# An attention layer and a layer of 160 experts on one core: one after the other, or in bursts between head groups

## The chip, the cores and the metric

The kernel runs on one core of a Trainium2 chip. The core has a tensor engine (PE, whose weight loads the profile lists as PEld), a vector engine (DVE), a scalar engine (ACT), a general engine (POOL) and a sync engine (SP), which here only issues transfers. [...] The metric is the device time of the kernel in microseconds (us): 3245.87 us as the median of three runs (3244.12 to 3246.43). Smaller is better.

## The reference

Sixteen batches of 512 tokens with 128 channels pass through one transformer block. Shifts, scales and gates of both halves come from a small conditioning vector. First comes causal attention with 16 heads of 8 channels, and then a mixture of 160 experts, of which each token takes 8, and one shared expert. All is in float32.

```python
mod = (_silu(L0_c) @ L0_wmod).reshape(L0_c.shape[0], 6, 1, -1)
sa, ca, ga, sb, cb, gb = (mod[:, k] for k in range(6))      
h = _layernorm(x) * (1 + ca) + sa
# attention: qkv = h @ qkv_w.T + qkv_b, rotary q and k, causal softmax, out @ proj_w.T + proj_b
x = x + ga * attention(h)
h = _layernorm(x) * (1 + cb) + sb
probs = sigmoid(h @ router_w.T + expert_bias)                 # 160 experts, inner width 64
top_w, top_idx = top_k(probs, 8)
top_w = 2.5 * top_w / (sum(top_w) + 1e-9)
routed = sum over the 8: top_w * (silu(h @ w_gate[e].T) @ w_down[e].T)
x = x + gb * (routed + silu(h @ w_gate_shared.T) @ w_down_shared.T)
```

## The kernel before

**Attention.** `attention` runs over 64 head groups: 16 batches, each with four groups of four heads. `prepare` makes one batch ready two batches ahead: normalized rows, transposes, q, k and v, the rotary turn, and q and k split into three bfloat16 parts, which go out to DRAM (`parts`). `fetch` brings the parts of one head group back, repeated over the partitions, into one of four pairs of tiles (`NREP = 4`, `qrep` and `krep`), with six transfers on SP. For each head group the program writes, in turns, the scores of this group with the causal mask (L363, L370), their exponentials on ACT (L373), the scores of the group two ahead (L317, L324) for their row maxima on DVE (`maxima`, L329), and the weighted sum of v (`weighted`, L382). `shift` puts the maxima back as extra rows of q. `collect` divides by the sums, and `project` applies the output weights and the gate and adds to x. The scores live in three PSUM tiles of two banks (tag `s`). One bank (tag `o`) serves the small transposes, one (`av`) the weighted sums.

**Experts.** `experts` runs when the attention is over, and its pools take over PSUM: four banks with tag `m`, and two tiles of two banks with tag `u`. The 16 batches form four groups of four. For each batch `route` normalizes, finds the top eight experts and computes the shared expert. `place` sorts a group's tokens by expert: every pair of experts gets whole blocks of 128 slots, at most `NK` = 207 blocks a group. For every block of 128 tokens POOL scatters the rows to their slots in DRAM (`xg`), eight indirect transfers a block (L740). `compute` then takes four blocks of slots at a time, a quad, through five stages: `load` from `xg`, `turn` (transposes, L782, copied by DVE, L784), `up` (the gate weights of the pair and two router columns, L790; then DVE's small operations L801 to L806, the Silu on ACT, L809, and the weighting, L810 and L812), `back` (transposes, L819, copied by ACT, L821) and `down` (L826, copied by ACT, L834, and stored to `yg`). Different stages of five quads are written in each step. Gate and down weights of all experts (`wg`, `wd`) lie in SBUF. PE reads the numbers of the expert pairs into registers. `combine` gathers each token's eight rows back by eight indirect transfers on POOL (L848), sums them (L858), weights them and stores the result.

```python
for i in range(-2, NQ + 3):
    for stage, q in (("load", i + 2), ("turn", i), ("up", i - 1), ("back", i - 2), ("down", i - 3)):
        if 0 <= q < NQ:
            getattr(quads[q], stage)()
    next(beside, None)
drain(beside)
```

What sets the order: the program is unrolled, and the generators of this loop decide what stands beside what. `beside` is the placing of the next group and the routing of the one after it, later also the combining of the group before. The scatter of `x` slots needs a cleared `xg`; 18 zero fills (L119) stand on SP before the first parts are stored.

Of the kernel before, what the change touches and what calls it, by code (L numbers as in the profile page):

```python
# [19 lines left out]
NB = 16  # L20
# [9 lines left out]
NREP = 4  # L30
# [5 lines left out]
NGR = 4  # L36
GB_ = NB // NGR
TB = GB_ * NBLK
TOPK = 8

NK = TOPK * TB + NC - 1
# [7 lines left out]
OFF = [sum(S - P * a for a in range(i)) for i in range(NBLK + 1)]  # L49
# [3 lines left out]
def block_kernel(ctx: ExitStack, tc: tile.TileContext, t: dict, out: bass.AP):  # L53
    nc = tc.nc

    const = ctx.enter_context(tc.tile_pool(name="const", bufs=1))

    stats = ctx.enter_context(tc.tile_pool(name="stats", bufs=4))
    early = ExitStack()
    early_pool = early.enter_context(tc.tile_pool(name="early", bufs=1))  # L60

    def load(name, shape, dt=FP, rows=False, pool=const):
        dst = pool.tile(shape, dt, tag=name, name=name)
        nc.sync.dma_start(out=dst, in_=t[name].partition_broadcast(P) if rows else t[name])
        return dst


    x = const.tile([P, NB * NBLK, D], FP, tag="x", name="x")

    def load_x(eng, b):  # L70
        eng.dma_start(
            out=x[:, b * NBLK : (b + 1) * NBLK, :],
            in_=t["x"][b].rearrange("(n p) d -> p n d", p=P),
        )

    load_x(nc.gpsimd, 0)
    cT = load("cT", [D, NB])
    wmod = load("wmod", [D, 6 * D], pool=early_pool)
    c = SimpleNamespace(
        ident=load("ident", [P, P]),  # L80
        wqk=load("wqk", [D, 2, 2, D], pool=early_pool),
        bqk=load("bqk", [D, 2, 2], pool=early_pool),
        wv=load("wvT", [D, D], pool=early_pool),
        bv=load("bv", [P, D], rows=True, pool=early_pool),
        turn=load("turn", [D, 2, S], pool=early_pool),
        identb=load("identb", [P, P], BF, pool=early_pool),
        mask_q=load("mask_q", [P, P], BF, pool=early_pool),
        mask_k=load("mask_k", [P, P], BF, pool=early_pool),
    )
    for b in range(1, NB):  # L90
        load_x(nc.sync if b % 2 else nc.gpsimd, b)
    c.wproj = load("wprojT", [D, D], pool=early_pool)
# [11 lines left out]
    c.blocks = load("blocks", [P, NK])  # L104
    c.slots = load("slots", [P, NK])
    c.wg = const.tile([D, NC, P + 2], FP, tag="wg", name="wg")
    for k in range(8):
        sl = slice(k * NC // 8, (k + 1) * NC // 8)
        nc.gpsimd.dma_start(out=c.wg[:, sl, :], in_=t["wgT"][:, sl, :])


    xg = [tc.dram_tile([NK * P, D], FP, name=f"xg{i}") for i in range(2)]
    yg = [tc.dram_tile([NK * P, D], FP, name=f"yg{i}") for i in range(2)]
    zeros = early_pool.tile([P, 1, D], FP, tag="zeros", name="zeros")
    nc.gpsimd.memset(zeros, 0.0)
    for rows in xg:
        view = rows.rearrange("(p n) d -> p n d", p=P)
        for k in range(0, NK, 23):
            nc.sync.dma_start(out=view[:, k : k + 23, :], in_=zeros.broadcast_to([P, 23, D]))  # L119

    eps = const.tile([P, 1], FP, tag="eps", name="eps")
    nc.vector.memset(eps, EPS)


    mod = const.tile([D, 6, NB], FP, tag="mod", name="mod")
    with tc.tile_pool(name="pmod", bufs=1, space=PSUM) as pp, tc.tile_pool(
        name="smod", bufs=1
    ) as sp:
        sc = sp.tile([D, NB], FP)
        nc.scalar.activation(sc, cT, AF.Silu)  # L130
        pm = pp.tile([D, 6, NB], FP)
        for k in range(6):
            nc.tensor.matmul(
                pm[:, k, :], lhsT=wmod[:, k * D : (k + 1) * D], rhs=sc, start=True, stop=True
            )
        nc.vector.tensor_copy(mod, pm)
        for k in (CA, CB):
            nc.vector.tensor_scalar(mod[:, k, :], mod[:, k, :], 1.0, None, ALU.add)
        for k in (GA, GB):
            g = mod[:, k, :]  # L140
            sign = sp.tile([D, NB], FP)
            nc.vector.tensor_scalar(sign, g, 0.0, 2.0, ALU.is_ge, ALU.mult)
            nc.vector.tensor_scalar(sign, sign, 1.0, None, ALU.subtract)
            mag = sp.tile([D, NB], FP)
            nc.vector.tensor_scalar(mag, g, -1.0, None, ALU.mult)
            nc.vector.tensor_tensor(mag, mag, g, ALU.max)
            nc.vector.tensor_scalar(mag, mag, 0.25, None, ALU.max)
            nc.vector.tensor_tensor(g, sign, mag, ALU.mult)


    stat1 = const.tile([P, NB * NBLK, 2], FP, tag="stat1", name="stat1")
    stat2 = const.tile([P, NB * NBLK, 2], FP, tag="stat2", name="stat2")

    def moments(stat, n):
        six = stats.tile([P, 6], FP, tag="six", name="six")
        nc.vector.bn_stats(six, x[:, n, :])
        nc.vector.bn_aggr(stat[:, n, :], six)

    def invert(stat, sl):
        nc.scalar.activation(stat[:, sl, 1], stat[:, sl, 1], AF.Sqrt, bias=eps)  # L160
        nc.vector.reciprocal(stat[:, sl, 1], stat[:, sl, 1])

    def normalized(pool, stat, n):

        xn = pool.tile([P, D], FP, tag="xn", name="xn", bufs=4)
        nc.vector.tensor_scalar(
            xn, x[:, n, :], stat[:, n, 0:1], stat[:, n, 1:2], ALU.subtract, ALU.mult
        )
        return xn

    def first_statistics(blocks):
        for n in range(blocks.start, blocks.stop):
            moments(stat1, n)
        invert(stat1, blocks)

    first_statistics(slice(0, NBLK))
    attention(tc, c, x, mod, (stat1, stat2), (first_statistics, moments, normalized))
    early.close()
    invert(stat2, slice(0, NB * NBLK))
    experts(tc, c, t, x, mod, stat2, (xg, yg), out)  # L180


def drain(steps):
    for _ in steps:
        pass


def heads_of(v):
    return v[:, :, 0 : H * (HD + 1)].rearrange("p n (h e) -> p n h e", e=HD + 1)


def attention(tc, c, x, mod, statistics, normalization):

    nc = tc.nc
    stat1, stat2 = statistics  # L200
    first_statistics, moments, normalized = normalization
    with ExitStack() as ctx:
        sb = ctx.enter_context(tc.tile_pool(name="attn", bufs=2))
        pads = ctx.enter_context(tc.tile_pool(name="pads", bufs=1))
        ps = ctx.enter_context(tc.tile_pool(name="attn_ps", bufs=1, space=PSUM))

        def bank2():
            return ps.tile([P, 2, S], FP, tag="s", name="s", bufs=3)

        def bank(shape=None, dt=FP):  # L210
            return ps.tile(shape or [P, S], dt, tag="o", name="o", bufs=1)


        reps = []
        for i in range(NREP):
            pair = [
# [791 lines left out]
```

## Time and profile before

| | |
|---|---|
| median of three runs | 3245.87 us |
| the profiled execution, its own time | 3244.43 us |
| its span, from the first to the last instruction | 3243.1 us |
| mean granted clock of PE | 0.766 |
| busy: PE, DVE, POOL, ACT | 1758.9, 1439.5, 1061.9, 906.9 us |
| first exponentials' scores, and the last (L363) | 167.4 and 1147.4 us |
| scatters (L740) and gathers (L848) | 512 and 512, 977 and 968 ns each |
| quads | 208 (4 x 52) |
| loads of ACT's function tables | 36, 1283 ns each |

The profile is one execution. Busy time is the time in which an engine ran an instruction; matmuls are pipelined, so that several of them can overlap and a busy PE is not one at its peak. The rows of 40 digits cut the span into 40 slices of 81 us, each digit a busy share in tenths. The table of stretches gives, for chosen stretches of time, the busy time of each engine with its number of instructions in brackets, then the granted clock of PE, the share of the DMA engines and GB/s. The timeline lists single instructions: start, duration, engine, line, operation, output <- inputs, and in square brackets how long the engine was idle ahead of it and what ended that. "SPq" is a transfer issued by SP. The list of waits gives, for an instruction and what released it, the sum in us, how often, and the longest.

### The profile page before, as it was taken

Reading aid. Unit: us, or ns where it says so; the run is one execution under the profiler, and the core shown is the slowest. Engines: PE = TensorE matmul, PEld = TensorE weight load, DVE = VectorE, ACT = ScalarE, POOL = GpSimd, SP = SyncE. Lnnn points to the kernel's source line nnn. Section 1 sums busy time; section 2 is a strip of 40 time slices with the busy share of each in tenths; the row PEclk is TensorE's granted clock in tenths of the full one; section 3 lists DMA queues with packets and bytes.
Section 4 is the critical chain, followed back from the end, with each engine's and each line's share of the span. In section 5 each row is a group of like instructions: output and inputs, shape, how many; then the busy total and the mean of one; then the engine's idle time right before and its main releaser. Section 6 shows DMA issues by size and latency. Waiting matters only on the chain.

```text
span 3243.1 us, 37324 instructions
## 1 busy us (share of the span) xinstructions
PE 1758.9 (54%) x12772; PEld 1234.9 (38%) x12772; DVE 1439.5 (44%) x3719; ACT 906.9 (28%) x1448; POOL 1061.9 (33%) x1079
## 2 busy tenths in 40 slices
PE   2189889888988863141288235138137228336700
PEld 1044444444444432031187235137136117336600
DVE  4156666666766553140176344026336115235522
ACT  1044444544444441010055012015013004113400
POOL 3000000000000006726701664650662670662176
PEclk8589999999999965565599667559568569668855
DMA  9811111111111011111245234124234125334421
GB/s 285 232 53 48 58 52 46 59 52 48 52 59 50 31 65 43 51 57 60 71 140 151 71 94 120 55 77 127 54 90 134 62 68 157 82 93 132 136 58 49
DMA packets 348310, 277.55 MB, mean 86 GB/s; under 512 B 28032, under 2 KB 319584, under 8 KB 348128
## 3 DMA queue, kind: packets, MB, share of 16 engines
q1 hardware_dynamic: 313568, 200.56, 20.6%
q0 software_dynamic: 34560, 74.60, 8.0%
q8 instruction: 109, 1.79, 0.2%
q14 instruction: 73, 0.60, 0.1%
HBM read 142.54 MB, written 131.73 MB: 85 GB/s over the span
## 4 chain that ended last, share of the span: by engine, by line
PE 37%; another core or an unknown queue 20%; issue 13%; DVE 11%; ACT 7%; POOL 6%; SPq 4%; DMA 2%; ACTq 0%; DVEq 0%; POOLq 0%
PE av L382 8%; POOL got L848 6%; PE m L826 4%; PE u L790 4%; ACT pT L373 4%; PE s L317 4%; PE s L363 3%; PE m L819 3%; SPq L119 3%; PE m L782 2%; DVE s L858 2%; PE s L248 2%; DVE mins L329 1%; PE o L397 1%
## 5 line engine op out<-in xcount | busy, mean ns | idle before, releaser
L848 POOL DMA_INDIRECT got<-yg,idx x512 | 495.6, 968 | 668.9 <-DMA yg<-y 359.0
L740 POOL DMA_INDIRECT xg<-h,idx x512 | 500.1, 977 | 405.9 <-issue 152.6
L329 DVE TENSOR_REDUCE mins<-s 128x2 f32<-128x1024 f32 (+3 forms) x512 | 418.6, 820 | 316.7 <-PE s L324 309.0
L373 ACT ACTIVATE pT<-s 128x1024 f32<-128x1024 f32 (+3 forms) x512 | 357.3, 703 | 280.9 <-PE s L370 273.3
L790 PE MATMUL u<-wg,xT 128*128 x1656 | 261.9, 303 | 315.7 <-DVE xT L784 126.8
L819 PE MATMUL m<-ident,su 128*128 128x128 f32 x828 | 149.1, 310 | 417.6 <-DVE su L812 186.4
L790 PEld LDWEIGHTS u<-wg,xT 128*128 128x128 f32 x1656 | 234.7, 215 | 326.0 <-issue 234.2
L282 POOL TENSOR_TENSOR rot<-rot 128x1024 f32<-128x1024 f32 x16 | 37.7, 2353 | 931.5 <-DVE rot L257 931.5
L821 ACT COPY hwT<-m 128x512 f32<-128x512 f32 x208 | 121.5, 584 | 757.5 <-remote 439.3
L317 PE MATMUL s<-krep,qrep 96*128 96x512 bf16 (+3 forms) x1024 | 262.5, 308 | 105.5 <-DMA krep<-parts 92.4
L382 PE MATMUL av<-pT,v 128*32 128x256 f32 (+3 forms) x2048 | 276.2, 444 | 1.3 <-ACT pT L373 1.3
L819 PEld LDWEIGHTS m<-ident,su 128*128 128x128 f32 x828 | 105.1, 159 | 446.1 <-issue 386.1
L826 PE MATMUL m<-wd,hwT 128*128 x1656 | 255.3, 305 | 21.3 <-issue 20.3
L363 PE MATMUL s<-qrep,krep 128*128 128x512 bf16 (+3 forms) x1024 | 258.2, 306 | 12.1 <-DVE mins L329 11.9
L784 DVE COPY xT<-m 128x512 f32<-128x512 f32 x208 | 141.7, 682 | 237.6 <-remote 163.1
L826 PEld LDWEIGHTS m<-wd,hwT 128*128 128x128 f32 x1656 | 237.3, 221 | 23.0 <-issue 20.9
L858 DVE TENSOR_REDUCE s<-got 128x128 f32<-128x1024 f32 x64 | 120.9, 1889 | 245.4 <-DMA got<-yg,idx 242.3
L324 PE MATMUL s<-mask_q,identb 128*128 128x128 bf16 x1024 | 208.9, 223 | 0.0
L370 PE MATMUL s<-mask_k,identb 128*128 128x128 bf16 x1024 | 205.1, 221 | 0.0
L809 ACT ACTIVATE su<-u 128x520 f32<-128x520 f32 x208 | 125.8, 605 | 235.5 <-DVE zi L806 98.4
L834 ACT COPY y<-m 128x512 f32<-128x512 f32 x208 | 121.2, 582 | 213.8 <-issue 146.5
L782 PE MATMUL m<-ident,xs 128*128 128x128 f32 x828 | 145.5, 305 | 57.0 <-issue 22.9
(154 smaller groups left out, 2303.6 us busy)
## 6 DMA issues: line engine op xcount, KB each, us to landing
xs<-xg SPq DMA_DIRECT2D x204, 256.0 KB
yg<-y SPq DMA_DIRECT2D x204, 256.0 KB
xg<-zeros SPq DMA_DIRECT2D x18, 1472.0 KB
qrep<-parts SPq DMA_DIRECT2D x192, 96.0 KB
krep<-parts SPq DMA_DIRECT2D x192, 96.0 KB
parts<-three SPq DMA_DIRECT2D x16, 768.0 KB
xg<-h,idx POOLq DMA_INDIRECT x512
got<-yg,idx POOLq DMA_INDIRECT x512
```

Source lines behind the costliest of these rows:

```text
L317: nc.tensor.matmul(sc[:, a, 0:n], lhsT=q[0:MROW, h, j * P : (j + 1) * P], rhs=k[0:MROW, h, 0:n], start=True, stop=False,)
L324: nc.tensor.matmul(sc[:, a, n - P : n], lhsT=c.identb, rhs=c.mask_q, start=False, stop=True)
L329: nc.vector.tensor_reduce(mins[gg][:, j, 2 * pr : 2 * pr + 2], sc[:, :, 0:n], AX.X, ALU.max, negate=True)
L363: nc.tensor.matmul(sc[:, a, 0:n], lhsT=k[:, h, i * P : (i + 1) * P], rhs=q[:, h, i * P : S], start=True, stop=False,)
L373: nc.scalar.activation(pT[:, 2 * pr : 2 * pr + 2, 0:n], sc[:, :, 0:n], AF.Exp, scale=SCALE)
L382: nc.tensor.matmul(av[HP * r : HP * (r + 1), i * P : S], lhsT=vs[b % 3][:, i, at : at + HP], rhs=pT[:, r, 0 : S - P * i], start=(i == 0), ...
L740: s = nc.gpsimd.indirect_dma_start(out=gr.xg[:, :], out_offset=bass.IndirectOffsetOnAxis(ap=gr.idx[:, j, k : k + 1], axis=0), in_=gr.h[:, ...
L782: nc.tensor.transpose(pt[:, j * P : (j + 1) * P], self.xs[:, j, :], c.ident)
L790: nc.tensor.matmul(pu[:, j, 0 : P + 2], lhsT=self.xT[:, j * P : (j + 1) * P], rhs=c.wg[:, bass.ds(self.pids[j], 1), :].rearrange("p o n -> ...
L819: nc.tensor.transpose(pt[:, j * P : (j + 1) * P], self.u[:, j, 0:P], c.ident)
L826: nc.tensor.matmul(py[:, j * D : (j + 1) * D], lhsT=self.hT[:, j * P : (j + 1) * P], rhs=wd[:, bass.ds(self.pids[j], 1), :].rearrange("p o ...
L848: nc.gpsimd.indirect_dma_start(out=got[:, k, :], out_offset=None, in_=gr.yg[:, :], in_offset=bass.IndirectOffsetOnAxis(ap=gr.idx[:, t0 + j ...
```

## The change

Attention and experts become one program with one set of pools. The batches form five groups of 3, 4, 4, 3 and 2. As soon as the last batch of a group has left the attention, it is routed and placed, its rows are scattered, and its quads are written into the program in bursts of up to five steps after a head group of a later batch (`order.work()`); what is left follows the last head group. `Order` decides when scatters, quads, gathers and sums are written. It reckons its own time: 3.5 us for each of the four parts of a head group, 3.4 for a quad step, 7.9 for a block of eight indirect transfers on POOL, and 4.0 for landing.

With this go the following edits:
- Three instead of four pairs of q/k tiles; the fetch for head group g+3 is written after head group g.
- Scores of 256 columns or fewer are put four heads to a tile instead of two: 384 reductions and 384 exponentials for 512 each.
- A quad's four PSUM tiles a step come from the three score tiles (`s`); `o` serves all small work. The tags `m` and `u` are gone.
- The down weights are no longer held in SBUF: each quad loads four pairs of them, 256 KB, on SP, from an address that SP reads into a register; PE reads a second set of four numbers.
- x, h and the residual of a batch are not held in SBUF: the rows of h and the residual go out to DRAM (`rows`, `rest`) and come back per block (`hs`) and per batch (`xr`).
- Slots are laid out so that a quad's rows are contiguous per partition (2 KB for 512 B), with six small operations a batch to make the addresses.
- A group has 32 blocks of slots a batch and 80 more, so that there are 44, 52, 52, 44 and 36 quads: 228.
- The rank of a token within its expert takes more matmuls (224 for 128) and fewer additions.
- Eight gathered rows are summed by three additions instead of one reduction.
- The zero fills of `xg` (16, L391) are written one after each head group from the second on; `rot` is summed by DVE instead of POOL.

The core of the diff:

```diff
-NREP = 4
+NREP = 3
-NGR = 4
+GROUPS = (3, 4, 4, 3, 2)
...
+    def score_tiles(n):
+        per = 2 if n > S // 2 else 4
+        for h0 in range(0, GH, per):
+            s = bank2().rearrange("p a t -> p (a t)").rearrange("p (h t) -> p h t", h=per)
+            yield range(h0, h0 + per), s
...
+    def scatter(gr):
+        for i in range(gr.size):
+            for j in range(NBLK):
+                h = sb.tile([P, D], FP, tag="hs", name="hs", bufs=3)
+                nc.sync.dma_start(out=h, in_=rows[gr.first + i][:, j, :])
+                for k in range(TOPK):
+                    s = nc.gpsimd.indirect_dma_start(out=gr.xg[0 : gr.nk * P, :], in_=h)
+                yield
...
         def turn(self):
-            _, self.pids = nc.values_load_multi_w_load_instructions(gr.pid of this quad, engines=[PE])
-            pt = bank()
+            (p0,) = self.numbers(SP, 0, 1, NC - 4)
+            self.wd = sb.tile([P, 4, D], FP, tag="wd", name="wd", bufs=4)
+            nc.sync.dma_start(out=self.wd, in_=t["wdT"][:, bass.ds(p0, 4), :])
+            self.pids = self.numbers(PE, 1, 4, NC - 1)
+            pt = wide()
...
         def up(self):
-            pu = ps.tile([P, 4, 256], FP, tag="u", name="u", bufs=2)
+            pu = bank2().rearrange("p a (j n) -> p (a j) n", j=2)
...
         def back(self):
-            pt = bank()
+            self.at = self.numbers(PE, 5, 4, 3)
+            pt = wide()
...
+    def attend(gg):
+        shifting = shift(gg + 1) if 1 <= gg and gg + 1 < NGG else iter(())
+        av = ps.tile([P, S], FP, tag="av", name="av", bufs=1)
+        last = None
+        for i in range(NBLK):
+            pT = sb.tile([P, GH, S - P * (i % 2)], FP, tag=f"pT{i % 2}", name="pT", bufs=1)
+            es = exponentials(gg, i, pT)
+            ms = maxima(gg + 2, NBLK - 1 - i) if gg + 2 < NGG else iter(())
+            next(es)
+            if last is not None:
+                weighted(gg, *last, av)
+            next(ms, None)
+            next(shifting, None)
+            slot()
+            drain(es)
+            drain(ms)
+            order.passed(3.5)
+            route_on(("any",))
+            slot()
...
+            last = (i, pT)
+        weighted(gg, *last, av)
+        until(lambda: collected)
+        avs = sb.tile([P, S], FP, tag="avs", name="avs", bufs=1)
+        nc.scalar.copy(avs, av)
+        soon.append(collecting(gg, avs))
+        if gg + 3 < NGG:
+            until(lambda: (gg + 3) // NG in ready)
+            fetch(gg + 3)
...
+    for gg in range(NGG):
...
+        attend(gg)
+        if g == NG - 1:
+            soon.append(projecting(b))
+        if clearing and gg >= 1:
+            clear(*clearing.popleft())
+        route_on(("other",))
+        for _ in range(5):
+            if not order.work():
+                break
+    while routes or routing or soon or placed or later or order.left():
+        route_on(("any", "other"))
+        slot()
+        order.work() or order.passed(1.0)
...
+class Order:
+    BLOCK = 7.9
+    QUAD = 3.4
+    LAND = 4.0
...
+    def passed(self, us):
+        self.now += us
+        while self.free <= self.now + self.BLOCK:
+            if self.scatters:
...
+            elif self.gathers and self.gathers[0][2] <= self.now and len(self.sums) < 2:
...
+            else:
+                break
+            self.free = max(self.free, self.now) + self.BLOCK
+        while self.sums and self.sums[0][0] <= self.now:
+            next(self.sums.popleft()[1])
+    def work(self):
+        if not self.computes or self.computes[0][2] > self.now:
+            return False
...
```

## The prediction

> **What bounds the kernel now.** I read the busy table first, then the forty slices, then busy time by stretch, then single instructions in order of time.
>
> ```profile
> PE 1758.9 (54%) x12772; PEld 1234.9 (38%) x12772; DVE 1439.5 (44%) x3719; ACT 906.9 (28%) x1448; POOL 1061.9 (33%) x1079
> PE   2189889888988863141288235138137228336700
> POOL 3000000000000006726701664650662670662176
> PEclk8589999999999965565599667559568569668855
> ```
>
> No engine is busy for more than 54% of the span, and the two rows of slices exclude each other: where POOL has a 6 or 7, PE has 0 to 3, and PE's 8s and 9s stand over POOL's 0s. Three of the stretches of 81 us, one from the attention, one of scatters, one of expert blocks (columns: PE, PEld, DVE, ACT, POOL busy, then clock, DMA share, GB/s):
>
> ```profile
> 972.00:1053.00 81.00, 72.21 (x579) 37.33 (x578) 49.15 (x90) 38.99 (x57) 2.35 (x1) 0.98 0.14 51
> 1296.00:1377.00 81.00, 9.13 (x28) 6.24 (x28) 8.47 (x31) 6.14 (x9) 61.77 (x64) 0.52 0.16 51
> 1701.00:1782.00 81.00, 70.38 (x556) 64.55 (x556) 54.42 (x191) 44.31 (x79) 8.15 (x9) 0.94 0.54 151
> ```
>
> Attention and expert blocks are bound by PE (0.89 and 0.87 of the stretch), the scatters and gathers by POOL. They take turns. What POOL costs is not its busy time but its cadence; two neighbours of the last gathers:
>
> ```profile
> 3085.72 0.95 POOL L848 DMA_INDIRECT got<-yg,idx  x1 [0.30 <-issue]
> 3086.98 0.95 POOL L848 DMA_INDIRECT got<-yg,idx  x1 [0.30 <-issue]
> ```
>
> 0.95 busy plus 0.30 idle is 1.26 us; a scatter is 0.97 + 0.30 = 1.27 us. So 1024 of them take 1297 us of POOL, against 1062 of busy time. A block of 128 rows (8 of them) takes 10.14 us.
>
> [...]
>
> **The change, part by part.** The order of instructions of the changed program says where each quad (four expert blocks of 128 slots) stands between the 64 head groups. None stand in head groups 0 to 22, 33 to 38 and 51 to 52. Some stand in 31: 23 to 32, 39 to 49, 53 to 62. Together 144 of 228 quads precede the end of the attention; 84 follow. I add up along PE, and let POOL replace it where POOL takes longer.
>
> *Start: 73 us.* The first exponentials now run at 167.4 us. The 18 zero fills ahead of them hold SP for 5.24 each, 94 us. They move to between head groups 1 to 16, one after each group's fetch, where the next group's PE work covers them; if not, 16 x 3 = 48 us come back.
>
> *Attention: 64 x 14.3 = 915 us.* Now (1147.4 - 167.4) / 64 = 15.3 us each. I take off 1.0, PE's own waits at the end of a group, which the change defers (over 800 us, 52 groups: 27.1 + 26.3 us):
>
> ```profile
> PE o L397 <- ACT avs L393: 27.1, 39, 0.7
> PE o L344 <- DVE att L404: 26.3, 39, 0.7
> ```
>
> The rotary sum's move from POOL to DVE (16 x 2.35 us to 32 x about 0.69), and its 128 fewer reductions and exponentials, stay beside PE: DVE is at 0.61 there.
>
> *Routing and placement: 65 + 25 us.* A batch's router, transposes and shared expert issue on PE in 4.3 us (0.67 + 0.44 + 1.08 + 0.97 + 1.09, from the dense stretch); 15 batches fall inside the attention. The 224 key matmuls (128 before) and the small chains of four groups: about 6 us a group.
>
> *Quads: 144 x 3.5 = 504 us.* PE at full clock issues one in 2.66 us:
>
> ```profile
> 1653.57 0.60 PE L782 MATMUL m<-ident,xs 128*128 128x128 f32 x4
> 1654.01 1.06 PE L790 MATMUL u<-wg,xT 128*128 x8
> 1654.90 0.60 PE L819 MATMUL m<-ident,su 128*128 128x128 f32 x4
> 1655.34 1.06 PE L826 MATMUL m<-wd,hwT 128*128 x8
> 1656.23 0.60 PE L782 MATMUL m<-ident,xs 128*128 128x128 f32 x4
> ```
>
> In the 120 us from 1640 the up matmuls number 296, 37 quads: 3.24 us each, routing included. Now quads lose their own PSUM tags (4 + 2) and share three tiles with the scores, four tiles a step. The second transpose reuses the up tile, which z, zi, the sum, the reciprocal (0.16 + 0.17 + 0.17 + 0.21) and the Silu (0.61) must leave first. From the up matmuls' start, 1.06 + 0.71 + 0.61 plus handovers of some 0.2 each is about 3.0, against 2.24 of issue: 0.4 to 1.0 us late. Bounds 3.0 and 4.3; I take 3.5. Each also adds a 256 KB load of down weights and a register load on SP (and a second on PE). The trace shows neither's time. [...] Weights come three steps ahead of their use. DMA carries 768 KB per 3.5 us, 220 GB/s; the first slice shows 285. The 20 quads more than before (228 for 208; padding) are in the count.
>
> *Edits beside other work.* SP issues 1480 transfers for 1083 (rows and residuals out to DRAM and back, 64 KB row loads, two stores of parts a batch for one, the table); outside POOL's dense stretches SP has room, 64 groups x 6 us of fetch and shift rows in some 1800. The gathered rows are summed by three additions (0.69 for 512 columns, less for 256 and 128) for a reduction of 1.89, so DVE loses nothing. If DVE or SP lacked that room, it would show as lag, and is bounded there.
>
> *Table loads: 31 x 2.3 = 71 us.* 140 loads for 36; Exp and Silu now alternate at every burst. Two loads at 1.28 per burst, of which PE feels most[...].
>
> *Fetches: 33 x 5.5 = 182 us.* With three q/k pairs instead of four, the load for group g+3 waits for PE's last scores of g, and the maxima of g+3 come as PE's third item in g+1. At the start one sees what a fetch takes:
>
> ```profile
> 139.56 0.85 SPq L303 DMA_DIRECT2D qrep<-parts  x1
> ...
> 143.39 0.68 SPq L306 DMA_DIRECT2D krep<-parts  x1
> ```
>
> Six issues, 4.5 us, and PE's first score at 150.4: 10.8 with another fetch behind it; alone I estimate 7 to 10.8. PE has about 4 us of other work ahead (weighted sums, one tile of scores, the deferred transposes). So 3 to 7 are left[...]. Behind a burst (5 x 3.5 us) the fetch is hidden: only the 33 groups without one pay.
>
> *POOL's lag: 60 us.* The order written into the program reckons 7.9 us a block; the trace says 10.14. Where blocks are dense SP (behind a row load that waits for POOL) and DVE (a sum that waits for its gather) hold up the queues. Group 1's scatters: 18 blocks, 183 us, against some 151 of PE work from the middle of head group 32 to the end of 39: 32. Group 2's: 16 blocks, 162, against 152: 10. Group 1's gathers: 162 against 147: 15. Bounds 0 and 130.
>
> *After the attention: 488 us.* POOL sets it. Behind the last four quads of group 2 (25 us) it has 80 + 64 + 48 + 96 + 64 = 352 scatters and gathers, 446 us, and from the last gather to the end it is 17 us as now (3226.5 to 3243.1). The 84 quads, 294 us, lie beside it: group 4's 36 (126 us) beside the last two gather runs but one (144 x 1.26 = 182).
>
> Sum: 73 + 915 + 65 + 25 + 504 + 71 + 182 + 60 + 488 = 2383. The profiled execution was 3244.4 for a span of 3243.1, and the median of the runs is 3245.9; add 3, and give **2390**.
>
> **The rivals.** *A: fetches and bursts are covered* (chance 0.15): scores buffered ahead, fetches at 7 us, quads at 3.2. Minus 130, 50, 43 and 40 of POOL's lag: 2120 to 2200. For it: in the dense stretch PE has hardly a gap. Against: [...] the q/k count fell.
> *B: the queues lock to POOL* (0.20): SP carries row loads, fetches, weights and stores in one line; each late scatter stops the next fetch, and with it PE. Inside the attention POOL has 84 blocks, 852 us; if a third of that stands alone instead of 60 us (284 - 60 = 224), and quads take 4.3 (144 x 0.8 = 115), it is 2720; with half of that, 2550. For it: SP's waits now (stores on ACT's copies 363 us, loads 315 us), already with fewer instructions.
> *C: slower than before* (0.02): the weight load with its register address makes each quad a serial trip on SP. It decides from (3243 - 2383) / 228 = 3.8 us more a quad, 7.3 in all; at 8.5 us the time would be 3520. [...]
> That nothing is interleaved is excluded by the instruction order.
>
> **How the numbers follow.** My case has 0.63, A 0.15, B 0.20, C 0.02. My own range is 2250 to 2560 (fetches 3 to 7 us, quads 3.0 to 4.3, lag 0 to 130: -82 to 50, -72 to 115, -60 to 70, not all at one end). The range given, 2230 to 2640, reaches into A and B and leaves some 0.2 out. A measurement of this kernel tells 0.2% from no change. Only C is slower: faster 0.97, same 0.01, slower 0.02.
>
> **What would show it.** POOL near 1.27 us per indirect transfer with few gaps after the attention's end, and that end near 1895 us. PE waiting for krep loads of some 5 us in groups 0 to 22, and none behind bursts. Quads 3.5 us apart. 140 table loads. DVE waiting for got. Wrong if the quads' spacing exceeds 4.3, if the start isn't near 75, or if SP's register loads take over 2 us.

## The result and the profile after

The changed kernel is slower: 3375.6 us median of 4 runs (3373.1 to 3378.7) against 3246.2 for the kernel before (3244.1 to 3253.1), a ratio of 1.0395, 95% interval 1.0377 to 1.0414. The profiled execution has a span of 3372.3 us. The prediction was 2390.

The page of the changed kernel, busy time and slices:

```profile
PE 1991.7 (59%) x13360; PEld 1335.4 (40%) x13424; DVE 1464.0 (43%) x4083; ACT 1066.0 (32%) x1546; POOL 1010.1 (30%) x1049
PE   4687753678885337558864556468527553374450
POOL 2000035100004640440025524530460545514436
PEclk8788875889997669779986678679759776597675
```

The quads now stand between the head groups, but the two rows still lean against each other: PE's 7s and 8s lie over POOL's 0s and 1, and where POOL has 4 to 6, PE mostly has 3 to 5. Two stretches of 84 us, one with scatters beside the attention, one without POOL (columns: PE, PEld, DVE, ACT, POOL busy, then clock, DMA share, GB/s):

```profile
505.80:590.10 84.30, 32.77 (x177) 16.97 (x177) 21.24 (x67) 15.55 (x19) 46.14 (x48) 0.59 0.16 53
843.00:927.30 84.30, 72.56 (x587) 54.33 (x590) 54.75 (x158) 47.55 (x73) 0.00 (x0) 1.00 0.48 157
```

In the first, no engine is busy for more than 0.55, DMA for 0.16. Something keeps work that is ready from starting. Single instructions, in order of time, just before that stretch, while POOL issues a scatter every 1.26 us from 461 to 501 (start, duration, engine, line; in brackets the idle time before and what ended it, where "remote" stands for a releaser that the profile couldn't name):

```profile
468.63 0.22 PE L277 MATMUL s<-mask_q,identb 128*128 128x128 bf16 x1
...
472.51 0.34 PE L622 MATMUL o<-m,onesb 128*128 128x160 bf16 x1
...
472.64 0.31 PE L323 MATMUL s<-mask_k,identb 128*128 128x128 bf16 x1
475.58 0.81 ACT L326 ACTIVATE pT<-s 128x768 f32<-128x768 f32 x1 [7.71 <-remote]
...
479.82 0.96 DVE L280 TENSOR_REDUCE mins<-s 128x2 f32<-128x768 f32 x1 [7.85 <-PE s L277]
...
505.06 0.49 DVE L626 TENSOR_TENSOR key<-o,first 128x320 f32<-128x320 f32 x1 [23.82 <-remote]
...
505.61 0.29 PE L622 MATMUL o<-before,onesb 128*128 128x160 bf16 x1 [26.27 <-DVE key L626]
...
505.82 1.02 ACT L326 ACTIVATE pT<-s 128x1024 f32<-128x1024 f32 x1 [29.43 <-remote]
```

L280 reads the scores that PE finished at 468.85 and starts at 479.82. L626 waits for one semaphore, the one that 2287 matmuls of PE update in this trace; the update that it needs rides on the matmul of 472.51. It starts at 505.06, 32 us after that matmul's end. The exponentials of 505.82 read scores finished at 472.95. In the other direction nothing is late: PE's L622 starts 0.05 us after L626's end. So what PE hands to ACT and DVE arrives late in this stretch, by 11 to 33 us, while POOL runs, and PE then waits for them (26.27 us ahead of L622). The chain of waits had a name for it. This is its line by engine, of the kernel before and of the changed one:

```profile
PE 37%; another core or an unknown queue 20%; issue 13%; DVE 11%; ACT 7%; POOL 6%; SPq 4%; DMA 2%; ACTq 0%; DVEq 0%; POOLq 0%
```

```profile
PE 38%; another core or an unknown queue 21%; DVE 11%; issue 11%; ACT 7%; DMA 7%; POOL 4%; SPq 2%; DVEq 0%; ACTq 0%; POOLq 0%
```

There is no other core here. A fifth of both spans had no releaser that the profile could name, and the prediction passed over it.

The trace also records when each semaphore update arrives. I matched PE's updates with the matmuls that carry them; "in a run" means that at least five transfers began in the 8 us ahead. Some update records are missing; the match gives each recorded one to a matmul, in order, so that the sum of the delays is as small as it can be.

| trace | PE updates in runs of transfers | over 1 us late | median |
|---|---|---|---|
| kernel before | 189 | 174 | about 13 us |
| changed kernel | 243 | 219 | about 8 us |

Outside the runs the median is 14 ns in both.

### The profile page after: what moved, and what is told of

It reads as the page before. It is cut to its first block, busy times and chain, and to the rows that moved or that the text cites. A ratio compares the mean times of both kernels' runs of the same rounds, so it can differ in the third digit from the quotient of the medians.

```text
span 3372.3 us, 41427 instructions
## 1 busy us (share of the span) xinstructions
PE 1991.7 (59%) x13360; PEld 1335.4 (40%) x13424; DVE 1464.0 (43%) x4083; ACT 1066.0 (32%) x1546; POOL 1010.1 (30%) x1049
## 4 chain that ended last, share of the span: by engine, by line
PE 38%; another core or an unknown queue 21%; DVE 11%; issue 11%; ACT 7%; DMA 7%; POOL 4%; SPq 2%; DVEq 0%; ACTq 0%; POOLq 0%
PE av L336 7%; PE s L746 5%; PE s L710 5%; PE s L270 5%; POOL got L780 4%; PE s L316 3%; DMA krep<-parts 3%; DVE mins L280 3%; PE s L703 2%; PE s L277 2%; PE s L323 2%; PE s L217 2%; PE s L739 2%; ACT y L754 1%
## 5 line engine op out<-in xcount | busy, mean ns | idle before, releaser
L658 POOL DMA_INDIRECT xg<-hs,idx x512 | 496.9, 971 | 1547.5 <-DMA krep<-parts 653.9
L280 DVE TENSOR_REDUCE mins<-s 128x2 f32<-128x1024 f32 (+3 forms) x384 | 397.3, 1044 | 517.5 <-PE s L277 327.5
L326 ACT ACTIVATE pT<-s 128x1024 f32<-128x1024 f32 (+2 forms) x384 | 333.8, 882 | 641.0 <-PE s L323 374.2
L746 PE MATMUL s<-wd,hwT 128*128 x1824 | 301.4, 316 | 205.2 <-DVE xT L705 83.5
L710 PE MATMUL s<-wg,xT 128*128 x1824 | 302.1, 315 | 145.3 <-issue 40.5
L336 PE MATMUL av<-pT,v 128*32 128x512 f32 (+3 forms) x2048 | 321.4, 483 | 85.6 <-ACT pT L326 84.6
L746 PEld LDWEIGHTS s<-wd,hwT 128*128 128x128 f32 x1824 | 264.7, 223 | 244.9 <-DVE xT L705 90.6
L710 PEld LDWEIGHTS s<-wg,xT 128*128 128x128 f32 x1824 | 260.3, 219 | 188.9 <-issue 57.3
L316 PE MATMUL s<-qrep,krep 128*128 128x384 bf16 (+3 forms) x960 | 251.1, 325 | 87.6 <-DVE mins L280 41.5
L739 PE MATMUL s<-ident,su 128*128 128x128 f32 x912 | 164.5, 310 | 196.1 <-issue 73.4
L703 PE MATMUL s<-ident,xs 128*128 128x128 f32 x912 | 162.0, 307 | 170.0 <-ACT hwT L741 67.9
```

The source lines that it names most:

```text
L280: nc.vector.tensor_reduce(mins[gg][:, j, heads.start : heads.stop], sc[:, :, 0:n], AX.X, ALU.max, negate=True,)
L316: nc.tensor.matmul(sc[:, a, 0:n], lhsT=k[:, h, i * P : (i + 1) * P], rhs=q[:, h, i * P : S], start=True, stop=False,)
L326: nc.scalar.activation(pT[:, heads.start : heads.stop, 0:n], sc[:, :, 0:n], AF.Exp, scale=SCALE)
L336: nc.tensor.matmul(av[HP * r : HP * (r + 1), i * P : S], lhsT=vs[b % 3][:, i, at : at + HP], rhs=pT[:, r, 0 : S - P * i], start=(i == 0), ...
L658: s = nc.gpsimd.indirect_dma_start(out=gr.xg[0 : gr.nk * P, :], out_offset=bass.IndirectOffsetOnAxis(ap=gr.idx[:, NBLK * i + j, k : k + 1] ...
L703: nc.tensor.transpose(pt[:, j * P : (j + 1) * P], self.xs[:, j, :], c.ident)
```

## The experiments

Two theories at the start. **Theory 1**: back-to-back indirect transfers on POOL hold up PE's handoffs, so POOL's time adds to the rest. **Theory 3**: the written order couples the engines (row loads on SP behind buffers that POOL must free, sums on DVE behind rows that POOL has yet to gather). Theory 2, traffic, is a variant of the first.

One fact is needed to read the numbers. Runs sent together share one chip and the kernel before. These groups fall in two settings: in some the kernel before has a median of 3244 to 3248 us, in others of 2958 to 2960. I call the first **late**, the second **prompt**, because that is how PE's updates behave in every trace that I matched (in runs of transfers, 393 of 432 over 1 us late in the two of the table, none of 1057 in two prompt ones). The expectations speak of two kinds of chip; that proved wrong, since one chip showed the prompt setting in one group and the late one in another. The first measurement was late. Compare within a setting.

**Chains of handoffs alone.** A small kernel with chains of 24 handoffs beside different backgrounds, in outline:

```diff
+for name, (f, n) in backs.items():      # nothing, gathers, scatters, plain loads, fills ...
+    tc.strict_bb_all_engine_barrier()
+    for k in range(n):
+        f(k % 64)                        # the background, on POOL or SP
+    for _ in range(24):                  # PE to ACT and back
+        nc.tensor.matmul(pa[:, 0:P], lhsT=ident, rhs=a[:, 0:P], start=True, stop=True)
+        nc.scalar.copy(a, pa)
```

> This kernel computes nothing of the reference: it runs four short chains (PE to ACT and back, PE to DVE and back, ACT to DVE and back, 24 rounds each; 96 matmuls of PE alone) one after another, each chain beside seven backgrounds: nothing, 40 indirect gathers on POOL, 40 indirect scatters on POOL, 40 plain loads of the same 64 KB issued by POOL, the same issued by SP, 100 fills on POOL, and gathers each followed by a fill. Theory 1 (a run of indirect transfers on POOL holds up what PE hands to ACT and DVE): the two chains with PE take at least twice as long beside gathers and scatters as beside nothing, until POOL's 40 transfers (about 50 us) are through, while ACT-to-DVE and PE alone stay within 20%; SP's loads and POOL's fills change nothing. Theory 2 (it is the traffic of 512 byte packets): the plain loads, from POOL or from SP, slow the chains as much as the gathers do. Theory 3 (neither; in the kernel it is the order of the queues): all chains stay within 20% beside every background.

It fell in the prompt setting (before 2958.1). Every step took 1.47 us from PE to ACT and 1.58 from PE to DVE, beside every background. Theory 1 had failed there, or needed what this group lacked. A second set, with a chain in which PE runs ahead:

> Computes nothing of the reference: the chains PE to ACT and back, PE to DVE and back and ACT to DVE and back as before, and a fourth one in which PE runs ahead as in the kernel (48 tiles of four matmuls over four PSUM buffers, drained by ACT and DVE in turn, so that one semaphore update of PE stands for several matmuls), each beside nothing, 40 indirect gathers, 40 indirect scatters, 40 plain loads of 64 KB from POOL, the same from SP, and gathers each followed by a fill of 0.56 us. On a chip of the second kind (before at 2958 us) all steps stay within 20% everywhere. On a chip of the first kind (before at 3246 us): theory 1 says that the chains with PE stretch from about 1.5 us a step to 5 us and more beside gathers and scatters, until POOL is through, while ACT to DVE stays at 1.2; if traffic is the cause, the plain loads do the same; if only updates that stand for several matmuls are late, only the fourth chain stretches; if none stretches, the cause needs something else that the kernel does.

Prompt again (2960.4), and flat again. The same kernel a third time:

> The same four chains beside the same six backgrounds as in the second set of chains (computes nothing of the reference), because that set ran on a chip where the kernel before takes 2960 us. If this one shows the kernel before at 3246 us: beside gathers and scatters the steps of the chains with PE stretch from 1.5 to 5 us or more if late updates need no more than PE and POOL's transfers; they stay at 1.5 if they need something else that the kernel does. If it shows 2960 us again, all steps stay within 20%.

This group was late (3244.3). Time in us of the 24 steps that one consumer takes, second set (prompt) / third set (late):

| background | PE to ACT | PE to DVE | ACT to DVE | PE ahead |
|---|---|---|---|---|
| nothing | 34.4 / 34.5 | 37.0 / 37.0 | 26.0 / 26.0 | 43.7 / 42.5 |
| gathers | 34.4 / **54.5** | 37.0 / **57.0** | 28.5 / 28.5 | 41.8 / **87.9** |
| scatters | 34.4 / **58.2** | 37.0 / **54.7** | 28.8 / 28.9 | 42.3 / **88.5** |
| plain loads, POOL | 34.4 / 34.5 | 37.0 / 37.0 | 26.0 / 26.0 | 43.6 / 41.8 |
| plain loads, SP | 34.4 / 34.5 | 37.0 / 37.0 | 26.0 / 26.0 | 41.8 / 41.8 |
| gathers, a fill after each | 34.4 / 34.5 | 37.0 / 37.0 | 27.7 / 27.8 | 41.8 / 41.8 |

The fourth chain beside gathers, third set, PE and DVE:

```profile
824.81 9.17 PE L99 MATMUL pd<-ident,all 128*128 128x128 f32 x80 [0.87 <-SPq L109]
...
829.55 0.69 DVE L104 COPY junk<-pd 128x512 f32<-128x512 f32 x1 [1.09 <-PE pd L99]
836.98 0.69 DVE L104 COPY junk<-pd 128x512 f32<-128x512 f32 x1 [6.74 <-remote]
837.73 2.07 PE L99 MATMUL pd<-ident,all 128*128 128x128 f32 x8 [3.75 <-DVE junk L104]
...
860.10 0.69 DVE L104 COPY junk<-pd 128x512 f32<-128x512 f32 x1 [22.43 <-remote]
```

It is the kernel's picture. At eight records a tile PE has finished tiles 0 to 9 by 833.98; DVE, which takes every second tile, starts on tile 8 at 860.10, and PE stands, its four buffers full. So in the late setting theory 1 holds, and it is narrow: not bytes (beside plain loads of the same 64 KB the chains with PE take 34.5 and 37.0 us, as beside nothing), not POOL's load (with a fill after each gather they take the same), not ACT-to-DVE handoffs (28.5 and 28.9 us late, 28.5 and 28.8 prompt), but runs of indirect transfers with nothing between them. Beside 24 gathers with a fill of 0.55 us after each, PE's handoffs are prompt, 34.5 us for the chain to ACT against 54.5.

**The transfers cut to an eighth.** Changed kernel (the cut of the kernel before is the same edit in its two loops; in both, the sums read the one row that is left eight times over):

```diff
-                for k in range(TOPK):
+                for k in range(1):
                     s = nc.gpsimd.indirect_dma_start(
...
-                for k in range(TOPK):
+                for k in range(1):
                     nc.gpsimd.indirect_dma_start(
```

> The changed kernel with one of the eight indirect transfers of every block of rows, 128 instead of 1024 (seven eighths of the scattered and gathered rows are left out; the sums keep their size); the order of all else stays. Theory 1 (POOL's transfers add to the time whatever is written beside them): 3372 less 896 x 1.267 = 1135, about 2240 us, 2100 to 2400. Theory 3 (pace of the written order, heads of line on SP and DVE): part of it remains, 2500 to 3000. If the added quads, table loads and fetches were the cause, over 3000.

> The kernel before with one of the eight indirect transfers of every block of rows (seven eighths of the scattered and gathered rows are left out; the sums keep their size). Theory 1: 3243 - 1135 = 2108, 2000 to 2200 us, and some 100 below the same cut of the changed kernel, because the interleaving brings nothing and its additions remain. If the interleaving is worth something once POOL is out of the way, the changed kernel's cut is the faster one.

2381.0 and 2125.4 us, both in the ranges of theory 1. The busy lines of the two pages, changed kernel first:

```profile
PE 1832.5 (77%) x13360; PEld 1230.2 (52%) x13424; DVE 1450.9 (61%) x4083; ACT 1060.7 (45%) x1545; POOL 142.2 (6%) x153
```

```profile
PE 1657.5 (78%) x12708; PEld 1147.9 (54%) x12772; DVE 1380.4 (65%) x3719; ACT 903.8 (43%) x1446; POOL 194.2 (9%) x183
```

Without most of POOL's work PE is the busiest engine in both, and the interleaved program is 256 us slower by itself, where some 100 were expected; 175 of them are busy time of PE. Which of the many edits makes them wasn't tested. The difference to the whole kernels is what the 896 transfers cost, 1135 us of POOL at 1.267. Set against the late traces, it is 3243.1 - 2123.2 = 1120 us in the kernel before, 99% of their time, and 3372.3 - 2379.2 = 993 in the changed kernel, 87%. So the interleaving hides 127 us more, costs 256, and ends 129 behind. (That the parts add up to the difference of the spans is arithmetic. The cuts ran prompt; before's attention, where POOL issues no transfer, ends at 1148.2 us in the late trace and at 1148.3 in a prompt one, so I use them for both.)

**The order's pace.**

```diff
-    BLOCK = 7.9
+    BLOCK = 10.2
```

> The changed kernel with 10.2 us instead of 7.9 in the order's own reckoning for a block of eight transfers, the cadence that the traces show; nothing else is changed. Theory 3 (the order issues transfers faster than POOL takes them, and SP and DVE stand behind them): 2500 to 3000 us. Theory 1: the transfers add their time wherever they are written, 3310 to 3440 us.

3020.6 us, ratio 1.0211 (1.0194 to 1.0228), prompt. Waits and slices of this version:

```profile
PE   3677785478888657677887377677676537555500
POOL 2000007500004751441017720556612660444476
DVE got L810 <- DMA got<-yg,idx: 446.1, 64, 34.0
```

Here POOL's 4 to 7 mostly do stand under PE's 5 to 7, and yet it is no faster than before. All its handoffs are prompt (no update of PE in its trace is over 1 us late); DVE waits 446 us for gathered rows, once a block. The measured time lies between the ranges of the two theories; that of theory 1 was reckoned from the late time and says nothing in this setting.

**Both kernels again, for traces.**

> The changed kernel once more, unchanged, on the chip of these runs, where the kernel before takes 2958 instead of 3246 us and where, in the traces of the first four runs, every semaphore update of PE arrives within 1 us. Theory 1 as first stated (POOL's transfers hold up what PE hands on) would be a trait of the first chip alone; if it is the whole cause of the missing gain, the changed kernel is well below the kernel before here, 2100 to 2500. If the cause lies in the program (its order, the rows that POOL waits for, the sums that wait for POOL), the ratio stays at 1.02 to 1.06: 3020 to 3140 us, and above the 3021 of the version that reckons 10.2 us a block.

> The kernel before, unchanged, for its trace on this chip: 2950 to 2970 us. If the late handoffs were what kept PE idle beside POOL's transfers on the first chip, the stretches with dense transfers have PE at 0.4 and more here instead of 0.1.

Late: 3381.2 us, 1.0427 (1.0400 to 1.0455), and 3246.2. The expectation had assumed a prompt group; nothing follows but that the first result repeats.

**Row loads on POOL, and one part of the change alone.** In `scatter` the row of the next block is loaded by `nc.gpsimd.dma_start` ahead of the current block's transfers, instead of by `nc.sync.dma_start`. In the kernel before, the zero fills are issued after head groups 1 to 18:

```diff
-            nc.sync.dma_start(out=view[:, k : k + 23, :], in_=zeros.broadcast_to([P, 23, D]))
+            clears.append((view[:, k : k + 23, :], zeros.broadcast_to([P, 23, D])))
...
+            if gg and c.clears:
+                dst, src = c.clears.pop(0)
+                nc.sync.dma_start(out=dst, in_=src)
```

> The changed kernel with the 64 KB row loads ahead of the scatters issued by POOL itself, one block ahead, instead of by SP, so that nothing on SP stands behind a buffer that POOL has yet to free. POOL pays about 0.6 us for each of 64 loads, 38 us in all. If SP's queue is what couples the fetches, and so PE, to POOL (theory 3): 150 to 350 us less than the changed kernel, 0.94 to 1.00 of the kernel before. If the coupling lies in PE's late handoffs (theory 1): within 2% of the changed kernel, 1.02 to 1.06.

> One part of the change alone: the kernel before with its 18 zero fills issued one after each head group from 1 to 18 instead of ahead of everything on SP. By the step of the prediction the first exponentials come at 73 to 80 us instead of 167 and nothing of it comes back: 3246 - 89 = 3157, ratio 0.973, between 0.970 and 0.980. If the fills hold up the fetches that SP issues behind them (18 x 5.2 us), up to 94 us come back and the ratio is 1.00.

Prompt. The row loads: 3007.1, 1.0149 (1.0133 to 1.0166), in neither of the two ranges. A prompt version that leaves them on SP (the short fill below) takes 3004.5, so these loads are at most a small part; SP's other work wasn't taken away. The fills: 2930.3, 0.9900 (0.9884 to 0.9917), a miss. The scores of the first exponentials come at 109.7 us instead of 167.4, and five head groups between 12 and 20 last 5 to 7 us longer; 30 of the forecast 89 us remain.

**Both, and later sums.** `BLOCK` at 10.2, row loads on POOL, and each sum 8 us later:

```diff
-                self.sums.append((max(self.free, self.now) + self.BLOCK + self.LAND, sums))
+                self.sums.append((max(self.free, self.now) + self.BLOCK + 3 * self.LAND, sums))
```

> The changed kernel, unchanged. On a chip where the kernel before takes 2960 us, PE's updates arrive at once, and only the order of the queues and the added work are left: 1.01 to 1.03 times before (2990 to 3050), near the version with 10.2 us a block (1.021). If it is faster than before there, the late updates alone decided the sign on the first chip. Where before takes 3246 us: 1.04 again.

> The changed kernel with three waits on POOL loosened at once: row loads issued by POOL a block ahead, 10.2 us a block in the order's reckoning, and each sum of gathered rows written 8 us later, so that DVE stands less often before rows that have yet to land (544 us of DVE's waits in the version with the row loads alone). If DVE's order is what couples PE to POOL: 100 to 300 us less than the changed kernel, 0.92 to 0.99 of before on a chip of 2960 us. If it is not: within 2% of the version with the row loads alone, 1.00 to 1.03. On a chip of 3246 us theory 1 leaves it at 1.02 to 1.05.

Late: the changed kernel 3364.9, 1.0370 (1.0351 to 1.0389); the loosened one 3434.5, 1.0580 (1.0556 to 1.0604), slower, and above the 1.02 to 1.05 expected. In the late setting these three changes to the queues' order win nothing together. Whether later sums help in the prompt one wasn't tried.

**A fill behind every transfer.**

```diff
                     tc.add_to_no_dep_group(f"scatter{gr.g}", s)
+                    nc.gpsimd.memset(gap, 0.0)
```

> The changed kernel with a fill of 128x512 on POOL behind every indirect transfer, nothing else (in the third set of chains such a fill, 0.55 us, kept all of PE's handoffs on time: 1.47 us a step instead of up to 6.3; POOL then issues a gather every 1.67 us, so 1024 take 1710 us instead of 1297). Where the kernel before takes 3246 us: if late handoffs are what keeps PE idle beside the transfers, PE works beside them, and the time falls although POOL has 410 us more to do: attention's end near 2000 to 2200 instead of 2598, then 352 transfers, 588 us: 2600 to 2950 us, 0.80 to 0.91 of before. If something else keeps PE idle, the 410 us come on top: 3500 to 3800. Where before takes 2960 us no handoff is late, and the fills only cost: 3000 to 3400.

> The same with a fill of 128x8, some 0.1 us. If any instruction between two transfers is enough: below the version with the long fill, 2500 to 2850 us. If it takes the time of the long fill for the updates to get through: 3300 to 3450, as the changed kernel.

> The kernel before with a fill of 128x8 behind every indirect transfer. If the short fill is enough: the 1000 us after the attention's end at 1149 in which POOL issues transfers and PE stands still are used: 2850 to 3000 us, 0.88 to 0.93. If it is not: 3240 to 3400.

> The kernel before with three fills of 128x192 behind every indirect transfer, about 0.6 us together (a tile of 512 has no room there). POOL alone then needs 1024 x 1.85 = 1900 us after the first scatter at 1229: if the quads (975 us in the cut version) all lie beside it, about 3150, 3050 to 3250 us; if PE still stands still beside the transfers, 3246 + 590 = 3840, at least 3600.

All prompt, so these couldn't speak on the lateness: 1.0206, 1.0145, 1.0131 and 1.1140 (3297.4 us). In their traces PE's updates in runs are late in none of 627 (changed, short fill) and none of 430 (before, short fill). Nor did most fills stand where they were written. They depend on nothing, and the scheduler had gathered 756 of the changed kernel's 1024 long ones ahead of the first transfer, all of its short ones, and those of the kernel before in a few bunches; only in the last version does a fill, of 0.27 us, follow most transfers.

One of these runs is worth a second look. The changed kernel with short fills is through with them at 186 us, and its first transfer is at 461. From there on it is the changed kernel as it stands, in the prompt setting: **3004.5 us, 1.0145 (1.0128 to 1.0162)**. Late handoffs as the whole cause had asked for 2100 to 2500 here (the expectation of the first repeat above). Its slices and its wait for gathered rows (sum, how often, longest):

```profile
PE   3677786478888726578887557568747554465550
POOL 7630006500000773442007734540660547434436
DVE got L814 <- DMA got<-yg,idx: 462.9, 63, 35.0
```

With the spans of this setting the account of the cuts reads: the transfers cost the kernel before 2956.3 - 2123.2 = 833 us and the changed one 3011.0 - 2379.2 = 632. The interleaving hides 201 us more, costs the same 256, and ends 55 behind.

The last test pins the order: `tc.keep_in_program_order(...)` around every transfer and every fill of 128x512.

> The changed kernel with a fill of 128x512 strictly between every two indirect transfers (in the version before, the scheduler had bunched the fills behind runs of transfers). POOL then issues one transfer every 1.67 us, as in the spaced background of the chains. Where the kernel before takes 3246 us and the changed one 3370: if PE's late handoffs are the cause of the difference between the chips, this kernel takes about what the changed kernel takes where no handoff is late, 2950 to 3150 us, 0.91 to 0.97 of before, in spite of 410 us more of POOL's work; if they are not, 3400 to 3800. Where before takes 2960 us: 2990 to 3150, 1.01 to 1.06.

> The kernel of the run before once more: the changed kernel with one fill of 128x512 between every two indirect transfers, which took 3140 us on a chip where the kernel before takes 2959. Where the kernel before takes 3246 us and the changed one 3370: if late handoffs of PE are all that separates the two kinds of chip, 3100 to 3200 us, 0.95 to 0.99 of before, 230 us less than the changed kernel in spite of 410 us more of POOL's work; if they are not, 3400 us or more. Where before takes 2959 us: 1.06 again, and the question stays open for the whole kernel.

Prompt first: 3140.3, 1.0622 (1.0603 to 1.0641). Then late: **3142.7 us, 0.9697 (0.9664 to 0.9731)**, where the changed kernel has 1.037 to 1.043. POOL in the late run, then the slices:

```profile
475.18 0.96 POOL L660 DMA_INDIRECT xg<-hs,idx  x1 [0.16 <-issue]
476.14 0.55 POOL L672 MEMSET gap<- 128x512 f32 x1
476.85 0.96 POOL L660 DMA_INDIRECT xg<-hs,idx  x1 [0.17 <-issue]
```

```profile
PE   3778786478888544578886447668746654455520
POOL 2000019800004995671039966871983679766678
```

A transfer every 1.67 us, POOL busy for 1571 us instead of 1010, and the kernel some 230 us faster than the changed one; PE has 4 to 7 over POOL's 6 to 9 until the last two slices. Of 500 PE updates in runs, 5 are over 1 us late, median 14 ns. And the two settings, some 290 us apart for the kernel before, agree within 3 us for this one. This shows in the whole kernel what separates the settings: **late handoffs of PE beside back-to-back indirect transfers.** By the times of the two settings they cost the changed kernel 3375.6 - 3004.5 = 371 us and the kernel before 3246.2 - 2959.0 = 287. They are not the whole reason why the interleaving brings nothing: without them it still isn't faster (1.0145). The spaced version is the fastest measured in the late setting, 3% under the kernel before; in the prompt one it is 6% over.

## Why the prediction was wrong

| step | predicted | measured |
|---|---|---|
| scores of the first exponentials | 73 us | 81.0 |
| head group without quads or transfers | 19.8 | 22.9 (1 to 15), with three batches' routing (about 1 a group) |
| head group with five quads, no transfers | 34.1 | 35.1 (mean of 15) |
| spacing of quads in a burst | 3.5 (3.0 to 4.3) | 4.3 median |
| table loads | 140 | 140 |
| attention's end | 1895 | 1927 with an eighth of the transfers, 2297 in the prompt run, **2601** in the late one |
| after the attention | 488 | 452 with an eighth, 714 prompt, **771** late |

The whole sum, 2383, is within 4 us of the changed kernel with seven eighths of its transfers left out, 2379. So the prediction had, in effect, the transfers hidden behind other work. That the agreement is so close is luck. Without the 60 us of lag the attention was reckoned at 1835, and in the cut it took 92 more; the lag and the stretch after the attention were too high by about as much, 60 and 36. Within a head group, too, the split was another. In groups 1 to 15 PE waits 2.1 us a group for `krep`, not 5.5, but it is busy for 17.3, against 13.6 before, with a granted clock of 0.87 instead of 0.99. Quads stand at the upper bound of their spacing (the 0.2 us for a handover was an estimate; in the trace of the kernel before, DVE starts 0.04 us after the up matmuls that it waited for, the Silu 0.09 after DVE, DVE 0.03 after the Silu, medians), and yet five of them lengthen a group by what was reckoned; why isn't shown. C's mechanism didn't occur: 4.3 us a quad is far from its 7.3, and SP's register loads take 0.51 us (median); its chance of 0.02 rested on the author's estimate of these loads. Two readings were off and changed nothing: 1062 us is all of POOL's busy time, of which the transfers have 996, and the trace did show PE's register loads, 0.35 us (median).

The step that failed is *POOL's lag: 60 us*, with the bounds 0 and 130. In the late setting, that of the first measurement, the transfers lengthened the attention by 2601 - 1927 = 674 us, 588 transfers at 1.15 us: nearly all of their POOL time. The second is *After the attention: 488 us*, which had everything else "beside" the 446 us of 352 transfers. With an eighth of them that stretch still takes 452, and the others add 319. Together (706 + 283) that is the 989 between 2383 and 3372.

Not all of it is lateness. In the prompt setting, with every handoff on time, the transfers still add 370 us to the attention and 262 after it, 632 of the 993. Why is open. Inside the attention DVE waits 178 us for gathered rows there, against 58 in the cut; that is a candidate, but no run takes these waits away in this setting. So late handoffs are the smaller part of the 993, 361.

Under both lies the reading of the slices: "They take turns" was taken for an order that a new program could change. But the kernel before already writes its scatters and gathers beside quads (`beside`), and its slices exclude each other there too. The transfers' time stood alone in spite of the order, 99% of it late and 73% prompt. *B* came nearest, coupling to POOL, but named SP's queue, and of that queue the row loads, the part that was tested, are not it; and it stopped at 2720. The one rival on the slower side was C, with 0.02. "The transfers' time stays additive" was missing, and with it the 0.97 for faster was far too sure.

That work bound by PE and work bound by POOL gain by interleaving was the author's estimate, and no run shows it in general: in the late setting the changed kernel takes 1.04 of the kernel before and the spaced version alone is below it (0.97), and in the prompt one all interleaved versions lie at 1.01 to 1.06.

## What to carry to other kernels

Before reckoning what an interleaving hides, look for a stretch where the old program already writes the two kinds of work side by side. If the engines exclude each other there, find out why first. A large share of the chain without a named releaser need not be noise: follow three of its waits instruction by instruction, and compare when the producer ended with when the consumer started. A cut of the suspected resource in both versions gives both terms, what is hidden and what the change costs by itself. Compare it with whole kernels of the same setting.

## What the runs showed of the hardware that was not expected

- In the late setting, beside runs of indirect transfers 1.25 to 1.27 us apart, PE's recorded semaphore updates, and with them the starts of what waits for them, come late: 174 of 189 by over 1 us in the kernel before, 219 of 243 in the changed one, by up to 45 us in the chains and up to 63 in the kernel before. In the PE-to-ACT chain the first 18 steps are on time, then steps reach 6.3 us. The recorded updates of ACT and DVE are not delayed (median 9 and 11 ns in runs, in the repeated kernel before), though there more than half have no record; the ACT-to-DVE chain, as fast late as prompt (28.5 us beside gathers in both), says the same. Transfers 1.67 us apart, with a fill between them, delay next to nothing (5 of 500 updates).
- What makes a setting is open. It is not the chip alone, as said. In late traces update records are missing as well (DVE: 3428 updates, 3089 records in the kernel before; none are missing in the prompt cut of it). They do not always go with late updates: in the spaced version records are missing too in the late setting (3817 updates of DVE, 3524 records), and there PE's updates came on time (5 of 500 late). Every run here was recorded, so that none shows the kernel unrecorded.
- ACT-to-DVE steps grow from 1.11 to 1.25 us beside the transfers in both settings, and to 1.32 beside POOL's fills alone (first set). A fill of 128x512 takes POOL 0.55 us.
